# Key features on both halves of the partitions, scalings folded into constants, and another first product in the first MLP unit

## The chip, the cores and the metric

The kernel runs on one core of a Trainium2 chip. The metric is the device time of one execution in microseconds. Before the change it is 2621.38 us, the median of three runs from 2621.16 to 2624.04 us.

## The reference

There are two layers on an image x of two batches, 512 channels and 32 x 32 pixels. The first is a deformable attention with eight groups of 64 channels, followed by an MLP; the second is a plain attention over 1024 pixels. What matters here, cut down:

```python
# layer 0, per batch; 8 groups g of 64 channels; q is (64, 32, 32) in each group
q   = grouped_1x1(bn1(x), qw)
off = gelu(depthwise_6x6_stride_4(q) + b)             # (64, 8, 8)
off = tanh(einsum('bchw,oc->bohw', off, off_pw_w)) * 4.0   # o = x, y offset of 64 keys
vx, vy = gx + off[:, 0], gy + off[:, 1]
nx, ny = 2 * vx / 7 - 1, 2 * vy / 7 - 1
kv = grid_sample(bn1(x), (nx, ny))                    # bilinear at (nx + 1) * 16 - 0.5
k, v = grouped_1x1(kv, kw), grouped_1x1(kv, vw)
pos  = grid_q - (nx, ny)                              # grid_q = 2 * qx / 31 - 1, for x and y
bias = sign(pos) * log1p(abs(pos))                    # the "features" of a key
bias = relu(bias @ w1 + b1); bias = relu(bias @ w2 + b2)   # 2 -> 128 -> 128
bias = bias @ w3 + b3                                 # one number per pixel and key
out  = softmax(q.T @ k * 64**-0.5 + bias) @ v
x = x + out_w @ out + out_b
x = x + mlp_w2 @ gelu(mlp_w1 @ bn2(x) + mlp_b1) + mlp_b2   # 512 -> 2048 -> 512
# layer 1
q, k, v = linear(x); x = x + Wp @ (softmax(q k.T / sqrt(512)) v) + bp
```

pos has one x and one y part. Per group there are 32 pixel columns or rows times 64 keys of each, so 64 rows (32 for x, 32 for y) by 64 keys hold all features of a group. The 2 -> 128 -> 128 -> 1 network then runs on every pair of 1024 pixels and 64 keys.

## The kernel before

The program has four stages. Times in this section are those of the profiled execution.

**Head (0 to 37 us).** The weights of layer 1 are multiplied together on TensorE (`weights`, L589; products at L595), and beside that the first group pair goes through `chain(0)`.

**Main loop (37 to 1890 us, L886 to L930).** It has 256 steps, each with four keys of one group. A step does: the second half of the last step's sums (L888), moves and accumulating adds by DMA (L889), the broadcast load of the next table of features once in four steps (`load_tables`, L640, from the DRAM buffer `fdr`), the first network layer by one VectorE instruction (`st_layer1`, L676), the second by 32 TensorE matmuls with four ScalarE evictions behind them (`st_layer2`, L693, L703, L705), and its sum on VectorE (`st_sum`, L713). A group takes 16 steps.

Beside this runs background work, a generator `later()` (L556). It advances by one piece per step, up to its next `yield`: in each of the first 60 steps, then in three steps of four (L903 to L905). It prepares the next keys. `CHAINS` (L26) divides the eight pairs of groups into five chunks: two of one pair, then three of two. A pair is two groups of 64 channels on the two halves of the 128 partitions. For each chunk `later` runs

- `chain(ci)` (L320 to L477): the products for q, the depthwise convolution, Gelu into `gof` (L406), the products for the offsets (L418), Tanh into `th` (L428), `place_keys` (L439), the distances `pos` (L453), Abs, the log1p with a correction term (L456 to L469), and the write of the features to `fdr` (L470);
- `sample(ci)` (L479 to L554): the bilinear weights from `th` (L485 to L500), the gather as products with them (L513 to L533), and the products for k and v (L544, L547).

With K pairs in a chunk, n = 128 K. `th` is laid out as [partitions, 3, 2K groups, 64 keys]: the placed x, the placed y, and in the third part the values for the features, of all 2K groups side by side. The features themselves are made from `th[0:64, 2]` alone: 64 partitions (32 columns and 32 rows of pixels) by n elements.

`place_keys` multiplies by 4 and adds the key's grid place (L441), then scales by 2/7 and subtracts 1 (L446); L453 takes this from the query's grid place `gq`; L485 turns the placed keys into pixel coordinates. In chunk 0 the third part is placed first and the other two after the features have been sent off (L473).

There is also softmax work (`softmax_steps`, L831), in pieces too, one per step or so.

**Output projection and MLP (1890 to 2260 us).** The MLP runs in eight units, two batches times four quarters of the hidden layer. The products of a unit's first layer (`layer1`, L1089) are two-level Strassen-Winograd. `twice` (L141) lists them: three sets of seven products, each of which needs weights `w1x` and `w1e` (`w1e` are inner sums that are gathered by DMAs of GpSimd, `load_inner`, L986) and sums of the input `xb` and `xe`. A set's seven products lie at times 7g + t, by `STEPS`:

```python
    STEPS = ((0, 1), (1, 2), (3, 6), (4, 5), (6, 7), (9, 4), (12, 3))   # L139: (t, product)
```

so sets 0 to 2 start at 0, 7 and 14, and "fills" are put between by their own times. Products 1, 6, 7 and 4 are evicted by ScalarE (L166 to L176), and 2, 5 and 3 are added by VectorE. Some products share a PSUM bank: 6 and 7 (and 4) add on to the bank of product 1 once that has been read. The last fill, `second` (L1124, time 21), is the one plain product in `layer1` that needs no inner weights, w[0] by xb[0]: eight matmuls of 512 columns. It is added to c11, and Gelu makes the first quarter of the hidden layer from it. The other sets give the further quarters, by `done` (L1110). Then comes `layer2` (L1133). In the first unit of a batch, `xe` is still being summed by the fills `part(1)` and `part(2)`.

**Attention of layer 1 (2260 to 2622 us).** The change does not touch it.

[...] `tc.issue_after(i)` fixes where an instruction is put in that order. Instructions that are not ordered so are placed by the scheduler by their data.

Of the kernel before, what the change touches and what calls it, by code (L numbers as in the profile page):

```python
# [8 lines left out]
F32 = mybir.dt.float32  # L9
AF = mybir.ActivationFunctionType  # L10
ALU = mybir.AluOpType
# [3 lines left out]
P = 128  # L15
# [4 lines left out]
J = 64  # L20
NSL = 16
KT = 16
# [35 lines left out]
def conv_seq_kernel(ctx: ExitStack, tc: tile.TileContext, x, xt, kst, pst, cst, vec, wsm, outw, w1, w2, wl, wlt, brow, out):  # L58
    nc = tc.nc
# [30 lines left out]
    fdr = [dp.tile([2 * len(g), 4, 2 * W, KT], F32, name=f"fdr{i}") for i, g in enumerate(CHAINS)]  # L90
# [115 lines left out]
    ph = php.__enter__()  # L206
    with tc.tile_pool(name="lp", bufs=2) as lp:
# [45 lines left out]
        jg = cs[:, 0:192].rearrange("p (i j) -> p i j", i=3)  # L253
        gq = cs[:, 192:193]
        hb = ph.tile([P, 10], F32, name="hb")
        nc.gpsimd.tensor_scalar(hb[:, 0:9], cs[:, 193:202], -1.0, -0.5, ALU.mult, ALU.add)
# [16 lines left out]
        perm, place = pw_[:, 256:384], pw_[:, 384:512]  # L273
# [46 lines left out]
        def chain(ci):  # L320
            G = CHAINS[ci]
            K = len(G)
            (b, k0), n = G[0], 128 * K
            for i in range(K):
                k = k0 + i
# [5 lines left out]
                ps = flat("psq")  # L331
# [14 lines left out]
            acc = ph.tile([P, 3, K, 8, 8], F32, tag="acc", name="acc")  # L346
# [104 lines left out]
            ab, u, ln = (fe[0:64, i, :] for i in range(3))  # L451
            pos = thf[0:64, 2 * n : 3 * n]
            nc.vector.tensor_scalar(pos, pos, -1.0, gq[0:64], ALU.mult, ALU.add)  # L453
# [4 lines left out]
            if ci > 0:  # L458
# [4 lines left out]
            rc = acc.rearrange("p a k y x -> p (a k y x)")[0:64, 0:n]  # L463
# [15 lines left out]
        def sample(ci):  # L479
            G = CHAINS[ci]  # L480
            K = len(G)
            th = state[ci]
            gx = th[:, 0:2].rearrange("p i g j -> p (i g j)")

            nc.vector.tensor_scalar(gx, gx, 1.0, 16.0, ALU.add, ALU.mult)  # L485
            if ci > 0:
                yield

# [10 lines left out]
            nc.scalar.activation(hxf, th[:, 0].rearrange("p g j -> p (g j)"), AF.Abs, bias=hb[:, 0:1])  # L499
            nc.scalar.activation(hxf, hxf, AF.Relu, bias=1.0, scale=-1.0)  # L500
            yield
            gy = th[:, 1].rearrange("p (f k) j -> p f k j", f=2)
# [465 lines left out]
    with ExitStack() as top, tc.tile_pool(name="wp", bufs=1) as wp:  # L968
# [120 lines left out]
        def layer1(p, we, w, xb, xe, hm, others=()):  # L1089
# [40 lines left out]
            twice(mq, ((1, 6), (4, 7), (5, 3)), weights, moving, dest, done, ((21, second), *others))  # L1130
# [54 lines left out]
        for i, (b, p) in enumerate(units):  # L1185
# [11 lines left out]
            layer1(p, we, wa, xb, xe, hm, ((4, lambda: part(1)), (10, lambda: part(2))) if p == 0 else ())  # L1197
# [272 lines left out]
def _constants(np):  # L1470

    p = np.arange(P)
    kk = (p % 64)[:, None]
    j = np.arange(J)
    jx = np.broadcast_to((j % 8).astype(np.float32), (P, J))
    jy = np.broadcast_to((j // 8).astype(np.float32), (P, J))
    jm = np.where(kk < 32, jx, jy)
    gq = (np.float32(2.0) * (p % 32).astype(np.float32) / np.float32(31) - np.float32(1.0))[:, None]
    px = (p % 32).astype(np.float32)[:, None]
    py = ((p // 32)[:, None] + 4 * np.arange(8)[None, :]).astype(np.float32)  # L1480
    return np.ascontiguousarray(np.concatenate([jx, jy, jm, gq, px, py], axis=1), dtype=np.float32)
# [102 lines left out]
```

## Time and profile before

| | us |
|---|---|
| median of three runs | 2621.38 |
| the profiled execution, in all | 2623.41 |
| its span, from the first to the last instruction | 2621.6 |
| head, 0 to 37.2: TensorE / VectorE / ScalarE busy | 34.9 / 19.5 / 13.0 |
| main loop, 37.2 to 1895: the same | 1845.6 / 1805.7 / 1514.9 of 1857.8 |
| projection and MLP, 1895 to 2260 | 361.6 / 253.5 / 119.7 of 365.0 |
| layer 1, 2260 to 2621.6 | 355.1 / 232.6 / 98.1 of 361.6 |

The busy time of an engine is the time in which an instruction is executing on it; matmuls that overlap are counted once. Times below are microseconds from the start of the span. A line of the timeline has the start, the duration, the engine, the line of the kernel, the operation, output<-inputs, shapes, the number of instructions that are put together, and in brackets the time that the engine stood idle before it with what ended that. A line of the waits has who waited, for whom, and the sum, the number and the longest of these waits. A line of the table by stretch has the window, its length, then for TensorE, its weight loads, VectorE, ScalarE and GpSimd the busy time with the number of instructions, then the granted TensorE clock, the DMAs' share and GB/s.

The features' own operations in that execution: in a chunk of two the reciprocal L464 takes 1.74 us on 64 x 256, the others 0.2 to 0.42 us each, and L446 0.56 us on 128 x 768.

### The profile page before, as it was taken

Reading aid. Unit: us, or ns where it says so; the run is one execution under the profiler, and the core shown is the slowest. Engines: PE = TensorE matmul, PEld = TensorE weight load, DVE = VectorE, ACT = ScalarE, POOL = GpSimd, SP = SyncE. Lnnn points to the kernel's source line nnn. Section 1 sums busy time; section 2 is a strip of 40 time slices with the busy share of each in tenths; the row PEclk is TensorE's granted clock in tenths of the full one; section 3 lists DMA queues with packets and bytes.
Section 4 is the critical chain, followed back from the end, with each engine's and each line's share of the span. In section 5 each row is a group of like instructions: output and inputs, shape, how many; then the busy total and the mean of one; then the engine's idle time right before and its main releaser. Section 6 shows DMA issues by size and latency. Waiting matters only on the chain.

```text
span 2621.6 us, 48901 instructions
## 1 busy us (share of the span) xinstructions
PE 2597.2 (99%) x19648; PEld 1004.4 (38%) x19648; DVE 2311.3 (88%) x1462; ACT 1745.7 (67%) x2324; POOL 981.8 (37%) x1121
## 2 busy tenths in 40 slices
PE   9999999999999999999999999999999999999999
PEld 3332322233233233322233332332355665646556
DVE  7999999999999999999999999898776587666656
ACT  5887898888887888888887777777723242314041
POOL 1344544444445444444444454333332334200100
PEclk9999999999999999999999999999999999999999
DMA  5888988999999999899898999787777768400202
GB/s 190 174 191 186 213 183 184 195 200 201 189 191 194 188 204 195 180 190 201 186 202 181 196 193 193 163 181 166 160 198 162 153 139 177 90 16 0 73 0 57
DMA packets 177522, 428.27 MB, mean 163 GB/s; under 512 B 29936, under 2 KB 78208, under 8 KB 174608
## 3 DMA queue, kind: packets, MB, share of 16 engines
q0 software_dynamic: 107392, 273.09, 58.2%
q1 hardware_dynamic: 69472, 151.75, 17.4%
q8 instruction: 155, 2.54, 0.4%
q14 instruction: 71, 0.58, 0.1%
q10 hardware_dynamic: 432, 0.31, 0.0%
HBM read 82.16 MB, written 6.55 MB: 34 GB/s over the span
## 4 chain that ended last, share of the span: by engine, by line
PE 63%; DVE 12%; issue 10%; DMA 9%; POOL 4%; ACT 2%; DVEq 0%; SPq 0%; POOLq 0%; ACTq 0%
PE ps L693 37%; PE sw L1073 7%; PE sw L1234 7%; PE sw L160 6%; DVE h L676 5%; DMA u<-uc 3%; DVE ub L713 2%; POOL u L732 2%; PE sw L1332 2%; DMA u<-u 1%; PE psg L595 1%; DMA uc<-uc 1%; DVE hm L137 1%; DVE uo L713 1%; DMA w1e<-w1e 1%
## 5 line engine op out<-in xcount | busy, mean ns | idle before, releaser
L693 PE MATMUL ps<-h,cw 128*32 128x512 f32 x16384 | 1775.2, 593 | 10.8 <-ACT rx L703 7.7
L676 DVE CUSTOM_DVE_ANT_1 h<-ta,tb 128x4096 f32<-128x4096 f32 (+1 forms) x257 | 1130.1, 4398 | 20.8 <-PE ps L693 16.8
L693 PEld LDWEIGHTS ps<-h,cw 128*32 128x32 f32 x16384 | 525.7, 110 | 1229.3 <-issue 1132.9
L703 ACT ACTIVATE rx<-ps,sc 128x1024 f32<-128x1024 f32 x512 | 567.6, 1109 | 155.9 <-PE ps L693 97.5
L732 POOL DMA_DIRECT2D u<-u x397 | 410.1, 1516 | 14.6 <-DMA u<-ub 12.1
L705 ACT ACTIVATE ub<-ps,sc 128x1024 f32<-128x1024 f32 x256 | 307.8, 1202 | 84.0 <-PE ps L693 82.6
L713 DVE SCALAR_TENSOR_TENSOR ub<-rx,sc,ub 128x1024 f32<-128x1024 f32 x256 | 326.2, 1274 | 10.5 <-ACT ub L705 10.5
L715 POOL DMA_DIRECT2D uo<-ub x127 | 112.1, 883 | 584.2 <-DVE ub L713 536.7
L1073 PE MATMUL sw<-hm,w2t 128*128 128x512 f32 x448 | 193.9, 592 | 0.4 <-DVE hm L125 0.2
L705 ACT ACTIVATE uo<-ps,sc 128x1024 f32<-128x1024 f32 x128 | 153.9, 1202 | 42.4 <-PE ps L693 39.7
L713 DVE SCALAR_TENSOR_TENSOR uo<-rx,sc,uo 128x1024 f32<-128x1024 f32 x128 | 163.2, 1275 | 5.0 <-ACT uo L705 5.0
L732 POOL DMA_DIRECT2D u<-uc x126 | 126.8, 1269 | 19.4 <-DMA u<-uc 17.9
L715 POOL DMA_DIRECT2D uc<-ub x64 | 56.1, 877 | 199.7 <-DVE ub L713 158.9
L1073 PEld LDWEIGHTS sw<-hm,w2t 128*128 128x128 f32 x448 | 85.0, 190 | 104.8 <-issue 98.7
L137 DVE TENSOR_TENSOR hm<-hm,sw 128x512 f32<-128x512 f32 (+1 forms) x80 | 58.6, 737 | 74.4 <-PE sw L160 54.7
L715 POOL DMA_DIRECT2D u<-ub x64 | 55.4, 866 | 168.5 <-DVE ub L713 164.8
L732 POOL DMA_DIRECT2D uc<-uo x63 | 103.1, 1637 | 16.8 <-DMA uc<-uo 16.5
L732 POOL DMA_DIRECT2D uc<-uc x63 | 104.5, 1659 | 2.0 <-DMA uc<-ub 2.0
L1398 POOL DMA_DIRECT2D xs<-rs x6 | 7.2, 1200 | 258.1 <-DVE rs L137 258.1
L705 ACT ACTIVATE uc<-ps,sc 128x1024 f32<-128x1024 f32 x64 | 76.9, 1202 | 26.4 <-PE ps L693 16.6
L656 ACT ACTIVATE ta<-fb,vs 128x512 f32<-128x512 f32 (+1 forms) x65 | 89.2, 1376 | 6.5 <-DMA fb<-fdr 6.5
L732 POOL DMA_DIRECT2D u<-uo x63 | 83.3, 1322 | 24.7 <-DMA u<-uo 19.2
(294 smaller groups left out, 2624.9 us busy)
## 6 DMA issues: line engine op xcount, KB each, us to landing
uo<-ub POOLq DMA_DIRECT2D x127, 512.0 KB, 5.3
fb<-fdr SPq DMA_DIRECT2D x64, 512.0 KB, 6.1
u<-ub POOLq DMA_DIRECT2D x64, 512.0 KB, 6.7
uc<-ub POOLq DMA_DIRECT2D x64, 512.0 KB, 6.0
u<-u POOLq DMA_DIRECT2D x63, 256.0 KB, 7.0
u<-uo SPq DMA_DIRECT2D x63, 256.0 KB, 5.8
u<-uo POOLq DMA_DIRECT2D x63, 256.0 KB, 7.3
uc<-uc POOLq DMA_DIRECT2D x63, 256.0 KB, 8.0
```

The lines of the kernel that those rows point to most:

```text
L137: nc.vector.tensor_tensor(out, a, b_, op)
L160: nc.tensor.matmul(bank[:, e, :], w, x, start=(q in (1, 2, 5) and e == k == 0), stop=True, skip_group_check=True,)
L656: nc.scalar.activation(ta.rearrange("p j x -> p x j")[:, :, j0:j1], fb[:, 0, :, j0:j1], AF.Identity, bias=col("cb1"), scale=col("w1x"),)
L676: nc.vector._custom_dve(TENSOR_ADD_SAT, out=h1[:, y : y + step].rearrange("p y t x -> p (y t x)"), in0=a.unsqueeze(1).to_broadcast([P, ste ...
L693: nc.tensor.matmul(ps[32 * q : 32 * q + 32, h, :], cw2[:, 32 * z : 32 * z + 32], h1[:, 16 * h : 16 * h + 16, q, :], start=True, stop=True,)
L703: nc.scalar.activation(o, ps, AF.Relu, bias=sc[:, 4 + z : 5 + z])
L705: nc.scalar.activation(o, ps, AF.Relu, bias=sc[:, 4 + z : 5 + z], scale=sc[:, z : z + 1])
L713: nc.vector.scalar_tensor_tensor(r[1], r[0], sc[:, z : z + 1], r[1], ALU.mult, ALU.add)
L715: nc.gpsimd.dma_start(out=sums[s][1], in_=sums[s][3], accum_op=ALU.add)
L732: nc.gpsimd.dma_start(out=out, in_=in_, accum_op=ALU.add)
L1073: nc.tensor.matmul(ps[:, m, :], w[:, a, k, m * P : (m + 1) * P], x[:, b_, k, :], start=(k == 0), stop=(k == 1),)
L1234: nc.tensor.matmul(ps[:, m, :], w[:, a, k, c + m * P : c + (m + 1) * P], x[b_][:, k, :], start=(k == 0), stop=(k == nk - 1),)
```

## The change

**Layout of the features.** The six matmuls L418 become five: per half f of the partitions (groups of that half) one for x, one for y, both of 128 output rows, and one of 64 output rows for the features, which goes to the same half f of the partitions. `th` becomes [partitions, 5, m] with m = n / 2: x of both halves, y of both halves, and one slice whose lower and upper 64 partitions hold the feature values of the lower and upper groups. All operations of the features (L453 to L469) then run on 128 partitions by m elements instead of 64 by n. The write to `fdr` becomes two DMAs, one per half of the partitions.

**Constants.** The grid constants are scaled on the host, so that `place_keys` is one instruction per coordinate and gives pixel coordinates at once (128/7 times tanh plus 32/7 times the grid place); L446 and L485 go, and the `yield` behind L485 goes with it. The distances come in one instruction, -8/7 times tanh plus a constant that holds the query's grid place less that of the key. `gq` goes.

**First MLP unit.** `layer1` gets `early`, which is true for the very first unit alone. There the plain product is issued at time -1, ahead of all sets, and ScalarE copies it to the tile `r3` (in `first`); at time 13.5 `merge` adds it to c11 and issues the Gelu of that quarter. In the other seven units `second` stays at 21.

```diff
-        cs = ph.tile([P, 202], F32, name="cs")
+        cs = ph.tile([P, 201], F32, name="cs")
...
+            m = n // 2
             with tc.issue_after(marks[0]) if ci == 0 else nullcontext():
-                for i in range(3):
-                    for f in range(2):
-                        nc.tensor.matmul(
-                            ps[f][:, i * n // 2 : (i + 1) * n // 2],
-                            pw[i][64 * f : 64 * f + 64, :],
-                            gof[64 * f : 64 * f + 64].rearrange("p k j -> p (k j)"), start=True, stop=True,
-                        )
+                for f in range(2):
+                    r = slice(64 * f, 64 * f + 64)
+                    g = gof[r].rearrange("p k j -> p (k j)")
+                    for i in range(2):
+                        nc.tensor.matmul(ps[f][:, i * m : i * m + m], pw[i][r, :], g, start=True, stop=True)
+                    nc.tensor.matmul(ps[0][r, 2 * m : 3 * m], pw[2][r, r], g, start=True, stop=True)
             yield
...
-            th = ph.tile([P, 3, 2 * K, J], F32, tag="th", name="th")
-            thf = th.rearrange("p i g j -> p (i g j)")
+            th = ph.tile([P, 5, m], F32, tag="th", name="th")
             for f in range(2):
                 nc.scalar.activation(
-                    th.rearrange("p i (f k) j -> p f i (k j)", f=2)[:, f],
-                    ps[f][:, 0 : 3 * n // 2].rearrange("p (i m) -> p i m", i=3), AF.Tanh,
+                    th[:, f : 5 - f : 2, :], ps[f][:, 0 : (3 - f) * m].rearrange("p (i m) -> p i m", m=m), AF.Tanh,
                 )
...
             def place_keys(i0, i1):
                 for i in range(i0, i1):
+                    t = th[:, 2 * i : 2 * i + 2, :].rearrange("p f (k j) -> p (f k) j", j=J)
                     nc.vector.scalar_tensor_tensor(
-                        th[:, i], th[:, i], 4.0, jg[:, i].unsqueeze(1).to_broadcast([P, 2 * K, J]),
-                        ALU.mult, ALU.add,
+                        t, t, 128.0 / 7.0, jg[:, i].unsqueeze(1).to_broadcast([P, 2 * K, J]), ALU.mult, ALU.add
                     )
-                t = thf[:, i0 * n : i1 * n]
-                nc.vector.tensor_scalar(t, t, 2.0 / 7.0, -1.0, ALU.mult, ALU.add)
-
-            place_keys(2 if ci == 0 else 0, 3)
-
-            fe = ph.tile([P, 3, n], F32, tag="fe", name="fe")
-            ab, u, ln = (fe[0:64, i, :] for i in range(3))
-            pos = thf[0:64, 2 * n : 3 * n]
-            nc.vector.tensor_scalar(pos, pos, -1.0, gq[0:64], ALU.mult, ALU.add)
+
+            if ci > 0:
+                place_keys(0, 2)
+
+            fe = ph.tile([P, 3, m], F32, tag="fe", name="fe")
+            ab, u, ln = (fe[:, i, :] for i in range(3))
+            pos = th[:, 4, :]
+            posk = pos.rearrange("p (k j) -> p k j", j=J)
+            nc.vector.scalar_tensor_tensor(
+                posk, posk, -8.0 / 7.0, jg[:, 2].unsqueeze(1).to_broadcast([P, K, J]), ALU.mult, ALU.add
+            )
...
-            rc = acc.rearrange("p a k y x -> p (a k y x)")[0:64, 0:n]
+            rc = acc.rearrange("p a k y x -> p (a k y x)")[:, 0:m]
...
-            nc.sync.dma_start(
-                out=fdr[ci].rearrange("g c p j -> p (g c) j"), in_=ab.rearrange("p (g j) -> p g j", j=KT)
-            )
+            for f in range(2):
+                nc.sync.dma_start(
+                    out=fdr[ci][f * K : f * K + K].rearrange("g c p j -> p (g c) j"),
+                    in_=ab[64 * f : 64 * f + 64].rearrange("p (g j) -> p g j", j=KT),
+                )
...
-            gx = th[:, 0:2].rearrange("p i g j -> p (i g j)")
-
-            nc.vector.tensor_scalar(gx, gx, 1.0, 16.0, ALU.add, ALU.mult)
-            if ci > 0:
-                yield
-
+            gx = th[:, 0:4].rearrange("p i m -> p (i m)")
...
-        def layer1(p, we, w, xb, xe, hm, others=()):
+        def layer1(p, we, w, xb, xe, hm, others=(), early=False):
...
-            twice(mq, ((1, 6), (4, 7), (5, 3)), weights, moving, dest, done, ((21, second), *others))
+            def first():
+                ps = mq.tile([P, 2, 512], F32, tag="ps2", name="sw")
+                product(w, xb)(ps, 0, 0)
+                nc.scalar.copy(r3, ps)
+
+            def merge():
+                plus(c11, c11, r3)
+                gelu(0, c11)
+
+            plain = ((-1, first), (13.5, merge)) if early else ((21, second),)
+            twice(mq, ((1, 6), (4, 7), (5, 3)), weights, moving, dest, done, (*plain, *others))
...
-            layer1(p, we, wa, xb, xe, hm, ((4, lambda: part(1)), (10, lambda: part(2))) if p == 0 else ())
+            layer1(p, we, wa, xb, xe, hm, ((4, lambda: part(1)), (10, lambda: part(2))) if p == 0 else (), i == 0)
```

More of the change, by code (lines that the diff above doesn't have):

```diff
@@ L253, in conv_seq_kernel @@
         jg = cs[:, 0:192].rearrange("p (i j) -> p i j", i=3)
-        gq = cs[:, 192:193]
         hb = ph.tile([P, 10], F32, name="hb")
-        nc.gpsimd.tensor_scalar(hb[:, 0:9], cs[:, 193:202], -1.0, -0.5, ALU.mult, ALU.add)
+        nc.gpsimd.tensor_scalar(hb[:, 0:9], cs[:, 192:201], -1.0, -0.5, ALU.mult, ALU.add)
         uo = vp[:, NCH : 2 * NCH, :]
@@ L498, in sample @@
             hxf = hx.rearrange("p f k j -> p (f k j)")
-            nc.scalar.activation(hxf, th[:, 0].rearrange("p g j -> p (g j)"), AF.Abs, bias=hb[:, 0:1])
+            nc.scalar.activation(hxf, th[:, 0:2].rearrange("p f m -> p (f m)"), AF.Abs, bias=hb[:, 0:1])
             nc.scalar.activation(hxf, hxf, AF.Relu, bias=1.0, scale=-1.0)
             yield
-            gy = th[:, 1].rearrange("p (f k) j -> p f k j", f=2)
+            gy = th[:, 2:4].rearrange("p f (k j) -> p f k j", j=J)
             for i, (b, k) in enumerate(G):
@@ L1472, in _constants @@
     p = np.arange(P)
-    kk = (p % 64)[:, None]
     j = np.arange(J)
[L1475 to L1478, printed above, removed]
+    jx, jy = (np.broadcast_to(v.astype(np.float32), (P, J)) for v in (j % 8, j // 8))
+    jm = np.where((p % 64)[:, None] < 32, jx, jy)
+    grid = np.float32(2.0) * (p % 32).astype(np.float32)[:, None] / np.float32(31)
     px = (p % 32).astype(np.float32)[:, None]
     py = ((p // 32)[:, None] + 4 * np.arange(8)[None, :]).astype(np.float32)
-    return np.ascontiguousarray(np.concatenate([jx, jy, jm, gq, px, py], axis=1), dtype=np.float32)
+    place = np.float32(32.0 / 7.0)
+    return np.ascontiguousarray(
+        np.concatenate([jx * place, jy * place, grid - jm * np.float32(2.0 / 7.0), px, py], axis=1), dtype=np.float32
+    )
 def _order(np):
```

## The prediction

> **What bounds the kernel now.** I read the busy line of the page first, then the table of busy time by stretch, then TensorE's own waits inside the main loop (40 to 1895 us), and last the timelines at the two places that the change touches.
>
> ```profile
> PE 2597.2 (99%) x19648; PEld 1004.4 (38%) x19648; DVE 2311.3 (88%) x1462; ACT 1745.7 (67%) x2324; POOL 981.8 (37%) x1121
> ```
>
> ```profile
> 400.00:600.00 200.00, 197.31 (x1862) 60.37 (x1854) 198.54 (x110) 166.76 (x228) 93.96 (x113) 1.00 0.92 194
> ```
>
> ```profile
> PE ps L693 <- ACT rx L703: 7.7, 13, 1.9
> PE ps L693 <- DVE h L676: 1.6, 2, 0.8
> PE pkv L544 <- issue: 1.0, 1, 1.0
> PE ps L693 <- ACT ub L705: 0.7, 2, 0.4
> ```
>
> TensorE is busy 99%, VectorE 97 to 99% of the loop's stretches (second number: PE; fourth: DVE). But the loop's end is set by TensorE: in 1855 us it stands still for only 11.5 us (7.7+1.6+1.0+0.7 and two smaller rows of 0.3 and 0.2). So work taken off VectorE in the loop is worth at most its part in those 11.5 us.
>
> The transition into the first MLP unit, TensorE:
>
> ```profile
> 1951.94 1.89 PE L160 MATMUL sw<-xe,w1e 128*128 128x256 f32 x8
> 1956.02 1.13 PE L160 MATMUL sw<-xb,w1e 128*128 128x256 f32 x4 [2.19 <-DMA w1e<-w1e]
> 1956.98 4.44 PE L160 MATMUL sw<-xb,w1x 128*128 128x256 f32 x12
> 1961.26 1.03 PE L160 MATMUL sw<-xe,w1x 128*128 128x256 f32 x4
> ```
>
> ```profile
> 1953.80:1957.40 3.60, 1.41 (x7) 1.25 (x7) 0.21 (x1) 0.00 (x0) 3.15 (x4) 1.00 0.39 52
> 1957.40:1960.80 3.40, 3.40 (x9) 2.66 (x8) 2.33 (x3) 1.17 (x2) 1.08 (x2) 0.50 0.87 148
> ```
>
> The reader is to see two losses: 2.19 us in which TensorE waits for the last inner weight, and right after it 3.4 us at a granted clock of 0.50 (third number from the end), in which 12 passes need 4.28 us instead of 12 x 0.214 = 2.57: another 1.7 us. Together 3.9 us.
>
> ScalarE and VectorE in the head, and ScalarE at the end of that MLP unit:
>
> ```profile
> 20.63 1.28 ACT L435 ACT_TABLE_LOAD   x1
> 21.93 0.20 ACT L435 ACTIVATE hb<-ones 128x1 f32<-128x1 f32 x1
> 22.04 0.29 ACT L456 ACTIVATE fe<-th 64x128 f32<-64x128 f32 x1
> ```
>
> ```profile
> 21.40 0.27 DVE L453 TENSOR_SCALAR th<-th,cs 64x128 f32<-64x128 f32 x1
> 22.70 0.28 DVE L462 SCALAR_TENSOR_TENSOR fe<-fe 64x128 f32<-64x128 f32 x1
> 22.91 0.94 DVE L464 RECIPROCAL acc<-fe 64x128 f32<-64x128 f32 x1
> ```
>
> ```profile
> 1965.78 0.60 ACT L172 ACTIVATE hm<-sw 128x512 f32<-128x512 f32 x1 [2.00 <-PE sw L160]
> 1966.39 1.28 ACT L1092 ACT_TABLE_LOAD   x1
> 1968.70 1.33 ACT L1092 ACTIVATE hm<-hm,vs 128x512 f32<-128x512 f32 x2 [1.02 <-DVE hm L137]
> ```
>
> [...] there is no load between a Gelu and the copies after it. [...] half the columns is less than half saved: here 128x64 takes 0.21 us (L402) and 128x128 0.28.
>
> **Head (chunk 0 of the features).** Removed from VectorE before the distances: L446 and L453 (0.22 and 0.27); the rest shrinks. But the Abs at 22.04 doesn't wait for them: L453 ends at 21.67, and ScalarE is held by the table load and its dummy until 22.04. So this fusion gains nothing there. Behind it: two ScalarE steps 0.05 shorter each (128 to 64 columns), four VectorE operations 0.07 shorter each, and the reciprocal. That takes 0.94 us at 128 columns and 1.74 at 256 in the loop, so 6.2 ns per column and about 0.54 at 64: 0.40 gained. Sum 0.1+0.28+0.40 = 0.8 us, so the write of fdr starts at 24.1 instead of 24.90. It is two DMAs now; the load of the first table waits for the first alone (its half holds the first group), and the second is issued beside that wait. [...] So the tables come 0.8 to 0.9 earlier. What is late next is TensorE: its products L595 stand before the loop, the last starts at 36.30 and would release the loop at 36.73, while L693 starts at 37.25 because of h. Gain 0.5 us (0.3 to 0.7). The six matmuls L418 now go by half, not in turn between halves: 12 passes took 0.8 us and I keep 0.8 (0.2 either way, inside the range).
>
> **Loop (chunks 1 to 4).** For a chunk of two: before, by rows of the trace at 439 to 467 us, 0.42+0.75+0.56+0.34+0.41+0.41+1.74+0.22+0.40+0.41+0.41 = 6.1 us of VectorE. After: two placings 0.75, the fused one 0.23, and at 128x128 0.28+0.94+0.15+3 x 0.28 = 2.2; together 3.2. So 2.9 us less, three times, and 1.6 for the single chunk: 10.3 us off VectorE. TensorE's stalls that follow such features while VectorE is behind are those at 875 (0.36), 927 (0.26), 935 (0.99) and 1276 us (0.31): 1.9. I take 1.5. The yield that goes with L485 moves all later background work one step earlier per chunk, four steps at the end. By the order of the built program this parts two clumps (in step 147 a tensor reduce of features and the softmax maximum stood together, 4.1 us; they become 2.9 and 1.2 four steps apart), makes one denser (steps 52 and 53: 1.45 and 2.69 against 53 and 54: 0.59 and 2.60), and saves one table load of 1.28 us on ScalarE near 412 to 428 us, where TensorE loses 2.6. I take 0.5 for these. Loop: -2.0. It isn't bounded well: at the good end half of the 11.5 us goes (-6), at the bad end new collisions come (+8, below). On SP one issue of 0.69 to 1.18 us becomes two of about half; SP only moves data that lands several microseconds ahead of its use, cost zero; its effect if that cover is gone lies in the +8.
>
> **First MLP unit.** The product without inner weights (8 passes x 0.43 = 3.43 us) now comes first. It is moved, not added. TensorE then reaches the late weight at 1953.8+3.4 = 1957.3, after it has landed at 1955.97: the 2.19 us and the 1.7 us of half clock go, and some 0.3 us of small waits of the first steps, now behind the cover: -4.2. Its eviction (about 1.0 us on ScalarE) is beside matmuls.
> But the bias step (merge, then Gelu) now stands in the middle. On ScalarE the program has, in this order: the eviction of product 7 of set 1, that of product 4 of set 1, the table load, two Gelus, and only then the first copy of set 2. TensorE's product 6 of set 2 adds into the bank that this copy must have read. TensorE has product 4 of set 1 just before it. Call the end of that T: eviction starts at T+0.2 (1961.26+0.86 to 1962.33), 0.60; table load 1.28; Gelus 1.33; copy 0.58; about 0.1 of semaphores: T+4.1. Merge on VectorE is ready at T+0.1 and doesn't matter. So TensorE stands for 4.1 us. Before, the copy came ahead of all Gelus and nothing waited. An idleness of 4.1 us will drop the clock again: 0 to 2.4 us, I take 1.3. Unit: -4.2+4.1+1.3 = +1.2 (from -0.2 to +2.4). Behind the stall, the program puts layer 2's first product between the last ones of layer 1, and no later operand comes late by my reckoning: the next unit's inner weights had 7 us to spare before their last product, and lose 2.
>
> **Sum.** -0.5-2.0+1.2 = -1.3 us. The profiled execution took 2623.4 us (span 2621.6 and 1.8 around it), 2.0 over the median 2621.4; 2623.4-1.3 = 2622.1, on the median 2620.1.
>
> **Rivals.**
> (A) The forecast: one stall of the first unit is replaced by another. 2620, own range 2616 to 2625. Chance 0.56.
> (B) The cover works: the copy isn't late, or TensorE's wait for it is under a microsecond. For it: the stall removed is in the trace, clock and all. Against it: ScalarE's order as built. -0.5-2.0-4.2 = -6.7: 2614.7. Chance 0.21.
> (C) Slower: the earlier background work meets the softmax work in the loop. A collision of that kind at 414 to 423 us cost TensorE 2.6; three more, one for each chunk of two (steps 52 to 54 most likely), are 7.8 in place of the -2.0: -0.5+7.8+1.2 = +8.5: 2630. It decides once the loop's stalls exceed the present 11.5 us by 4.5. For it: VectorE, ScalarE and the DMAs are all nearly full there. Against it: 10 us less of VectorE work, and clumps that are mostly parted. Chance 0.23.
> That the change doesn't do what it says is excluded by the built program: shapes are halved and the product is first.
>
> **How the numbers follow.** A measurement tells 0.2% (5.2 us) from no change. Faster than 2616.1: most of B and a tail of A, 0.25. Slower than 2626.6: most of C, a little of A, 0.22. Within: 0.53. The range 2613 to 2630 holds A, most of B and about half of C.
>
> **What would show it.** First L693 at about 36.7; the sum of TensorE's waits in the loop near 9.5; no wait for w1e in the first unit, a wait of about 4 us for ScalarE's copy L166 in its place, followed by a clock of 0.50; the VectorE groups of th and fe 10 us lighter. A first unit without that wait makes B right; a loop with waits above 16 us makes C right.

## The result, and the profile after

The changed kernel takes 2631.41 us, the median of five runs (2628.26 to 2637.49), beside 2621.38 us for the kernel before (2620.89 to 2624.04). The ratio is 1.0041, with an interval of 1.0025 to 1.0057: some 10 us slower. The forecast was 2620 with a range of 2613 to 2630. The change's runs also lie further apart than those of before. The profiled execution is the fastest of the five, 2628.26 us with a span of 2626.5, and so 3.2 us under its median, while that of before (2623.41) lay 2.0 over its own. Between the two profiled executions there are therefore only 4.9 us, half of what lies between the medians.

In the loop and the MLP the lines of the new kernel have numbers that are lower by four: L693 is now L689, L703 is L699, L1092 is L1088. First the busy line of the page, then TensorE's waits in the main loop (who, for whom: sum, number, longest), then ScalarE, the issue of the features' writes and TensorE around 466 us, all from the trace of the changed kernel:

```profile
PE 2599.4 (99%) x19648; PEld 1013.1 (39%) x19648; DVE 2300.7 (88%) x1446; ACT 1745.6 (66%) x2324; POOL 985.2 (38%) x1121
```

```profile
PE ps L689 <- ACT rx L699: 10.8, 10, 2.8
PE ps L689 <- DVE h L672: 1.6, 2, 0.8
```

```profile
461.44 1.19 ACT L701 ACTIVATE ub<-ps,sc 128x1024 f32<-128x1024 f32 x1
466.04 0.72 ACT L488 ACTIVATE sg<-th,edge 128x512 f32<-128x512 f32 x1 [3.40 <-DMA fdr<-fe]
466.79 0.72 ACT L489 ACTIVATE sg<-sg,edge 128x512 f32<-128x512 f32 x1
467.42 1.10 ACT L699 ACTIVATE rx<-ps,sc 128x1024 f32<-128x1024 f32 x1
```

```profile
461.87 1.99 SPq L470 DMA_DIRECT2D fdr<-fe  x2
```

```profile
468.56 6.64 PE L689 MATMUL ps<-h,cw 128*32 128x512 f32 x60 [2.80 <-ACT rx L699]
```

The same chunk in the trace of before, where L492 is the first instruction of `sample` on ScalarE:

```profile
467.10 0.65 SPq L470 DMA_DIRECT2D fdr<-fe  x1
474.80 0.72 ACT L492 ACTIVATE sg<-th,edge 128x512 f32<-128x512 f32 x1
```

VectorE has lost 10.6 us in all, close to the 10.3 that were computed for the loop. TensorE's waits for L699 have nevertheless gone from 7.7 to 10.8 us, and the longest, 2.8 us at 468.56, has a cause that the trace of before does not have at all. ScalarE stands still for 3.40 us ahead of L488, the first instruction of `sample`, until the write of the features to `fdr` has landed (the DMA is complete), and the eviction L699 that TensorE needs is queued behind it. `sg`, which L488 writes, has the tag "fe": it takes the buffer of the features, and the DMA still reads that buffer. The two writes were issued from 461.87 us on; the second landed at 465.93. Before, the write landed at 473.88, and L492 did not wait. In chunk 4 there is a second such wait, 1.69 us at 1234.

TensorE in the head, before:

```profile
19.15 0.89 PE L418 MATMUL sim<-gof,ws 64*128 64x64 f32 x12
19.96 2.84 PE L595 MATMUL psg<-wl_s 128*128 128x512 f32 x6
```

The same place in the changed kernel, and then its first MLP unit (TensorE, ScalarE, and a stretch of 3.4 us behind the wait):

```profile
19.35 0.66 PE L420 MATMUL sim<-gof,ws 64*128 64x64 f32 x4
19.94 0.33 PE L421 MATMUL sim<-gof,ws 64*64 64x64 f32 x2
20.19 0.66 PE L420 MATMUL sim<-gof,ws 64*128 64x64 f32 x4
20.78 0.33 PE L421 MATMUL sim<-gof,ws 64*64 64x64 f32 x2
21.03 1.55 PE L591 MATMUL psg<-wl_s 128*128 128x512 f32 x3
```

```profile
1964.60 1.03 PE L160 MATMUL sw<-xe,w1x 128*128 128x256 f32 x4
1969.43 3.56 PE L160 MATMUL sw<-xe,w1e 128*128 128x256 f32 x8 [3.80 <-ACT hm L166]
```

```profile
1965.66 0.60 ACT L176 ACTIVATE hm<-sw 128x512 f32<-128x512 f32 x1 [1.99 <-PE sw L160]
1966.28 1.28 ACT L1088 ACT_TABLE_LOAD   x1
1967.57 1.33 ACT L1088 ACTIVATE hm<-hm,vs 128x512 f32<-128x512 f32 x2
1968.81 0.56 ACT L166 COPY hm<-sw 128x512 f32<-128x512 f32 x1
```

```profile
1969.20:1972.60 3.40, 3.17 (x8) 2.55 (x9) 0.69 (x1) 0.76 (x2) 0.00 (x0) 0.50 0.00 0
```

The offset products are six before and after (the account of the change says five): x, y and features for each half, of which the change makes the two for the features 64 columns wide. Each shows as two passes, twelve in all. They take from 19.35 to 21.03 us, 1.68 us, where before they took 0.81 (19.15 to 19.96). The first MLP unit shows what was forecast: the eviction L176, the table load, two Gelus, and only then the copy L166, with TensorE waiting 3.80 us for it and a granted clock of 0.50 after it (the number before the last two in the line of stretches).

From the first to the last matmul of the loop before takes 1851.2 us, after 1854.4. From the first product L595 (L591) to the loop it is 29.91 and 30.77.

### The profile page after: what moved, and what is told of

Read it like the earlier page. It is cut to its first block, busy times and chain, and to the rows that moved or that the text cites. A ratio compares the mean times of both kernels' runs of the same rounds, so it can differ in the third digit from the quotient of the medians.

```text
span 2626.5 us, 48896 instructions
## 1 busy us (share of the span) xinstructions
PE 2599.4 (99%) x19648; PEld 1013.1 (39%) x19648; DVE 2300.7 (88%) x1446; ACT 1745.6 (66%) x2324; POOL 985.2 (38%) x1121
## 4 chain that ended last, share of the span: by engine, by line
PE 77%; DVE 10%; issue 7%; DMA 3%; POOL 2%; ACT 1%; DVEq 0%; SPq 0%; ACTq 0%; POOLq 0%
PE ps L689 48%; PE sw L1069 7%; PE sw L160 7%; PE sw L1240 7%; DVE h L672 3%; DVE ub L709 2%; PE sw L1016 2%; PE sw L1338 2%; DMA u<-uc 2%; POOL u L728 1%; PE psg L591 1%; PE sim L819 1%; DVE uo L709 1%; DVE hm L137 1%; PE psx L1316 1%
## 5 line engine op out<-in xcount | busy, mean ns | idle before, releaser
L689 PE MATMUL ps<-h,cw 128*32 128x512 f32 x16384 | 1773.6, 592 | 13.5 <-ACT rx L699 10.8
L689 PEld LDWEIGHTS ps<-h,cw 128*32 128x32 f32 x16384 | 531.3, 110 | 1224.7 <-issue 1139.5
L699 ACT ACTIVATE rx<-ps,sc 128x1024 f32<-128x1024 f32 x512 | 568.0, 1109 | 146.8 <-PE ps L689 116.0
L728 POOL DMA_DIRECT2D u<-uc x126 | 126.6, 1282 | 16.2 <-DMA u<-uc 14.4
L137 DVE TENSOR_TENSOR hm<-hm,sw 128x512 f32<-128x512 f32 x79 | 57.6, 732 | 78.4 <-PE sw L160 53.5
L701 ACT ACTIVATE u<-ps,sc 128x1024 f32<-128x1024 f32 x64 | 77.1, 1204 | 25.5 <-PE ps L689 19.3
```

The lines of the kernel that those rows point to most:

```text
L137: nc.vector.tensor_tensor(out, a, b_, op)
L689: nc.tensor.matmul(ps[32 * q : 32 * q + 32, h, :], cw2[:, 32 * z : 32 * z + 32], h1[:, 16 * h : 16 * h + 16, q, :], start=True, stop=True,)
L699: nc.scalar.activation(o, ps, AF.Relu, bias=sc[:, 4 + z : 5 + z])
L701: nc.scalar.activation(o, ps, AF.Relu, bias=sc[:, 4 + z : 5 + z], scale=sc[:, z : z + 1])
L728: nc.gpsimd.dma_start(out=out, in_=in_, accum_op=ALU.add)
```

## The experiments

Each time is the median of its runs; the ratio is to the kernel before, run beside it on the same chip. All experiments compute the whole reference. The names in the headings are used further on.

### The parts, one at a time

**b_early:** the kernel before with the MLP part of the change alone (`first` at -1, `merge` with its Gelu at 13.5, in the first unit).

> The kernel before with the MLP part of the change alone. Theory 1 (three separate causes; the first MLP unit costs what its trace shows, a wait of 3.8 us and a half clock of 3.4 us in place of 2.19 us and a half clock of 3.4 us): 1.0 to 1.6 us over before, about 2622.8, with the loop as before (first L693 at about 37.3). Rival (the MLP part is most of the change's 10 us, by something after the first unit): 2628 to 2631.

2625.03 us, 1.0013 (1.0006 to 1.0020): +3.6 us. The 3.80 us wait is there and the loop is as before, so the rival falls, but the cost is twice what was expected. The half clock lasts 6.83 us here, where the changed kernel's profile had 3.41.

**a_noearly:** the changed kernel without that part.

```diff
-            layer1(p, we, wa, xb, xe, hm, ((4, lambda: part(1)), (10, lambda: part(2))) if p == 0 else (), i == 0)
+            layer1(p, we, wa, xb, xe, hm, ((4, lambda: part(1)), (10, lambda: part(2))) if p == 0 else ())
```

> The changed kernel without the MLP part (features alone). Theory 1: 1.4 us under the changed kernel, about 2630, with the half clock and the 2.19 us wait for w1e back. Rival (the MLP part is most of it): about 2622.

2627.92 us, 1.0030 (1.0018 to 1.0041), 3.5 us under the changed kernel: the same size from the other side. The wait for w1e is back with 1.38 us, but no half clock follows it, against what was expected. This is followed up below.

**a_yield:** the changed kernel with the yield put back in `sample`.

```diff
             gx = th[:, 0:4].rearrange("p i m -> p (i m)")
+            if ci > 0:
+                yield
```

> The changed kernel with the yield of L485 put back into sample, nothing else. Theory 1 (the loop's loss is ScalarE's wait, at the head of its queue, until the two fdr writes have landed, because sg takes the buffer of fe; one step more lets them land first): no ScalarE wait on fdr over 0.5 us, the sum of TensorE's waits in the loop at most that of before (10.7 us), the time 2624 to 2627. Rival (the loop loses by the layout itself, the two writes or the longer products, and the yield is nothing): 2630 to 2632.

2625.62 us, 1.0016 (1.0010 to 1.0023): 5.8 us less from one bare `yield`, the largest single part. No wait for fdr is left on ScalarE, and TensorE's waits are

```profile
PE ps L691 <- ACT rx L701: 6.4, 9, 1.9
PE ps L691 <- DVE h L674: 1.5, 2, 0.8
PE ps L691 <- ACT ub L703: 0.7, 2, 0.4
```

in all 8.6 us, below the 11.5 of before. The theory holds.

**a_inter:** the changed kernel with the six offset matmuls in turn between the halves.

```diff
-                for f in range(2):
-                    r = slice(64 * f, 64 * f + 64)
-                    g = gof[r].rearrange("p k j -> p (k j)")
-                    for i in range(2):
-                        nc.tensor.matmul(ps[f][:, i * m : i * m + m], pw[i][r, :], g, start=True, stop=True)
-                    nc.tensor.matmul(ps[0][r, 2 * m : 3 * m], pw[2][r, r], g, start=True, stop=True)
+                for i in range(3):
+                    for f in range(2):
+                        r = slice(64 * f, 64 * f + 64)
+                        g = gof[r].rearrange("p k j -> p (k j)")
+                        if i < 2:
+                            nc.tensor.matmul(ps[f][:, i * m : i * m + m], pw[i][r, :], g, start=True, stop=True)
+                        else:
+                            nc.tensor.matmul(ps[0][r, 2 * m : 3 * m], pw[2][r, r], g, start=True, stop=True)
```

> The changed kernel with the five offset matmuls in turn between the halves of the partitions again (x of both, y of both, features of both). Theory 1 (matmuls on different halves run beside one another only if they alternate): they take about 0.8 us instead of 1.7 in the head, the first L689 comes about 0.8 us earlier (37.4 to 37.6), and 0.8 to 1.5 us less in all, about 2630. Rival (the later start is the launch's jitter or the two writes): 38.3 again and no change, 2631.

2629.78 us, 1.0034 (1.0021 to 1.0046). The first matmul of the loop is at 37.24 instead of 38.32, and from the first L593 to it there are 29.94 us instead of 30.77, so the head is as much shorter as was expected; whether for the reason given is tested by b_byhalf. The time is 1.6 us less, but with runs from 2627 to 2633 this can't be told from no change, and the waits for fdr were longer in this trace (4.35 and 2.38 us). Repeated without them below.

### The yield: a wait, or work that comes one step early?

**a_hxfirst:** the changed kernel with `hx` (in the buffer of `acc`) made before `sg` (in that of `fe`). As many yields as the changed kernel.

```diff
+            hx = ph.tile([P, 2, K, J], F32, tag="acc", name="hx")
+            hxf = hx.rearrange("p f k j -> p (f k j)")
+            nc.scalar.activation(hxf, th[:, 0:2].rearrange("p f m -> p (f m)"), AF.Abs, bias=hb[:, 0:1])
+            nc.scalar.activation(hxf, hxf, AF.Relu, bias=1.0, scale=-1.0)
+            yield
             sg = ph.tile([P, 3, 2, K * J], F32, tag="fe", name="sg")
...
             yield
             nc.vector.tensor_tensor(sg[:, 2], sg[:, 0], sg[:, 1], ALU.mult)
-            hx = ph.tile([P, 2, K, J], F32, tag="acc", name="hx")
-            hxf = hx.rearrange("p f k j -> p (f k j)")
-            nc.scalar.activation(hxf, th[:, 0:2].rearrange("p f m -> p (f m)"), AF.Abs, bias=hb[:, 0:1])
-            nc.scalar.activation(hxf, hxf, AF.Relu, bias=1.0, scale=-1.0)
-            yield
```

> The changed kernel with the two steps of sample changed over: hx (in the buffer of acc, free by then) first, then sg (in the buffer of fe, which the fdr writes still read). As many yields as the changed kernel, so all background work keeps its early step; only the wait for the landing goes. Wait theory (all of the 5.8 us that the yield gave are ScalarE's wait for fdr): 2625 to 2626, TensorE's wait near 468 us (2.8) gone. Shift theory (they come from the background work being one step early, as in TensorE's wait of 2.3 us at 414 us behind the Gelu of gof): 2631, that wait unchanged. If both share: about 2628, with the wait near 468 gone and that at 414 still there.

2625.88 us, 1.0018 (1.0010 to 1.0025), as with the yield. TensorE's waits in its trace:

```profile
PE ps L689 <- ACT rx L699: 7.7, 8, 2.3
PE ps L689 <- DVE h L672: 1.6, 2, 0.8
```

The 2.8 us wait is gone; the 2.3 us at 414, which is the early background work, is still there and costs nothing that shows in the time. (Before has 0.54 and 1.67 us at that place, nearly the same sum.) So the loss was the wait for the landing, and the shift was not.

**b_noyield:** the kernel before with the yield behind L485 taken out, so with the old layout, one write and a full VectorE.

```diff
             nc.vector.tensor_scalar(gx, gx, 1.0, 16.0, ALU.add, ALU.mult)
-            if ci > 0:
-                yield
```

> The kernel before with the yield behind L485 taken out, nothing else: sg then follows the one fdr write of the old layout at the same distance as in the changed kernel. Theory (the yield alone makes the loop's loss, the new layout and the two writes do not): a ScalarE wait for fdr of 2 us or more in one or two of the chunks of two, and 4 to 6 us over before, 2625 to 2628. Rival (it takes the two writes to make the landing late): no such wait, 2621 to 2622.

2631.46 us, 1.0039 (1.0027 to 1.0052): +10.2 us. One `yield`, and more than the expected 4 to 6. ScalarE waits for fdr for 3.61 us at 236 and 5.52 at 469, and behind these TensorE for 1.84 and 4.17 us; this is ScalarE in its trace:

```profile
462.28 1.19 ACT L703 ACTIVATE ub<-ps,sc 128x1024 f32<-128x1024 f32 x1
468.99 0.72 ACT L490 ACTIVATE sg<-th,edge 128x512 f32<-128x512 f32 x1 [5.52 <-DMA fdr<-fe]
```

The two writes and the layout are not needed for the loss. Why it is larger than in the new layout was not tested. The trace shows two half clocks in the loop, of 3.41 us each, after waits of 2.27 and 4.17 us, and ScalarE stands still ahead of L490 in the other two chunks of the loop as well: 1.90 us at 853, until 0.08 us behind the landing, and 2.70 us at 1240, where the landing (1240.26) and L485 on VectorE (1240.40) end almost together. L485 is not there in the changed kernel, so not all of this loss need be the landing.

### The order of the offset matmuls

**b_byhalf:** the six matmuls of before by half instead of in turn.

```diff
-                for i in range(3):
-                    for f in range(2):
+                for f in range(2):
+                    for i in range(3):
```

> The kernel before with its six offset matmuls by half instead of in turn, nothing else. Theory (each pass then runs alone; 0.9 us more of TensorE in the head and in the single chunk, about 1.1 in each chunk of two, and TensorE is the bound): 3 to 5 us over before, 2624.5 to 2626.5. Rival (only the head counts, in the loop the passes fall into waits): 0.8 to 1.6 over, 2622 to 2623.

2621.89 us, 1.0001 (0.9993 to 1.0009): no change that can be told. The 3 to 5 us of the theory are outside the interval (-1.8 to +2.4 us), and the reason given, that matmuls of different halves run beside one another only when they alternate, is wrong. TensorE in the head of this kernel:

```profile
19.85 1.16 PE L418 MATMUL sim<-gof,ws 64*128 64x64 f32 x12
20.94 1.55 PE L595 MATMUL psg<-wl_s 128*128 128x512 f32 x3
```

Twelve passes in 1.09 us, by half, beside 1.68 for the changed kernel's twelve. What the changed kernel has besides is a change of shape inside each half, from weights of 64 x 128 to 64 x 64 and back. Its lines above show it: four passes from 19.35, then L421 only at 19.94, then L420 of the other half only at 20.19. By the starts in its trace each change costs time: the last L420 of a half starts at 19.73 and the first L421 at 19.94, 0.20 us later, where within one shape the passes of a half follow by 0.11 (0.16 behind the first L420). From the last L421 (20.04) to the next L420 (20.19) it is 0.15. Nor do the two halves overlap there: the second half's first pass starts at 20.19, after the first half's last (20.04). In b_byhalf it starts at 20.13, ahead of three passes of the first half (20.23 to 20.46) that stand before it in the program, so by its starts TensorE did not keep strictly to the program's order there. In turn, all of one shape stand together and there is one such change between the products, where by half there are three. The trace of the features alone in turn (f_clean, below) has

```profile
19.78 0.66 PE L421 MATMUL sim<-gof,ws 64*128 64x64 f32 x8
20.37 0.33 PE L423 MATMUL sim<-gof,ws 64*64 64x64 f32 x4
20.63 1.55 PE L595 MATMUL psg<-wl_s 128*128 128x512 f32 x3
```

twelve passes in 0.85 us.

**f_clean:** the features part alone, with the yield and the matmuls in turn; the first MLP unit as before. **f_yield:** the same with the matmuls by half.

> The features part alone with its two losses mended (yield back, offset matmuls in turn), first MLP unit as before. It asks what 10 us less of VectorE work in the loop are worth. By the sum of the runs so far (all mended 2617.0, the MLP part with its Gelu at 21 worth 2.7 by the trace): 2619.7, so 1 to 2.5 us under before. Rival (VectorE's work is all beside TensorE's, worth nothing): 2621 to 2622.

> The features part alone with the yield back, the offset matmuls by half as in the changed kernel; beside it stands the run with the matmuls in turn (2618.45). Theory (in the new layout the order by half costs TensorE 0.85 us in the head and 0.6 to 1.0 in each chunk, as the traces show, and TensorE is the bound): 3 to 4.3 us more, 2621.5 to 2622.7. Rival (only the head's part counts): 0.9 more, 2619.3.

2618.45 us, 0.9989 (0.9983 to 0.9996), and 2622.08, 1.0003 (0.9995 to 1.0011). So the new features are worth 2.8 us, and the order by half in the new layout costs 3.6, more than all of it. By the traces it is 0.83 us in the head (29.94 from the first L595 to the loop, 30.77 by half) and 3.2 in the loop (1847.5 and 1850.7 us from its first to its last matmul), where each chunk's passes take 0.6 to 1.0 us longer.

**a_yinter:** the changed kernel with the yield and the matmuls in turn, its first MLP unit as changed.

> The changed kernel with the yield back and the offset matmuls in turn; the first MLP unit as changed. Theory: 3 to 4.3 us under the one with the yield alone (2625.6), 2621.3 to 2622.6; and 4 to 5 us over the one with the Gelu at 21 as well (2617.0). Rival: 0.9 under, 2624.7.

2621.61 us, 1.0001 (0.9993 to 1.0009), 4.0 us under a_yield: the same answer with the changed MLP unit. Over f_clean it is 3.2, the MLP part once more.

### The first MLP unit

**a_gelu21:** the changed kernel with the Gelu of c11 apart from its sum. **b_early21:** the same edit in b_early.

```diff
             def merge():
                 plus(c11, c11, r3)
-                gelu(0, c11)
-            plain = ((-1, first), (13.5, merge)) if early else ((21, second),)
+            plain = ((-1, first), (13.5, merge), (21, lambda: gelu(0, c11))) if early else ((21, second),)
```

> The changed kernel with the first unit's Gelu of c11 apart from the merge: the sum stays at 13.5, the Gelu goes to 21, behind the evictions of products 1, 6 and 7 of set 2. Theory (the wait of 3.80 us is the table load and the two Gelus ahead of the copy of product 1, and the half clock is that wait's): both are gone, no half clock from 1940 to 2000 us, 6 to 8 us under the changed kernel, 2623 to 2625. Rival (the wait moves to the later evictions or to layer 2, which reads that Gelu): a wait of over 2 us within 15 us after, 2628 to 2632.

> The kernel before with the MLP part alone, its Gelu at 21. By the trace of the first unit (50.17 us before, 47.48 with the product first and the Gelu at 21): 2.7 us under before, 2618.7, with one wait of 1.2 us for ScalarE's copy and no half clock in the unit. Rival (later units or the loop's end give it back): 2621.

2627.24 us, 1.0023 (1.0015 to 1.0030), and 2620.86, 0.9998 (0.9990 to 1.0007). In both, the 3.80 us wait shrinks to 1.16, as in this line of b_early21, and no half clock follows:

```profile
1963.85 1.99 PE L160 MATMUL sw<-xe,w1e 128*128 128x256 f32 x8 [1.16 <-ACT hm L166]
```

4.2 us are won in either kernel (2625.03 to 2620.86 without the new features). The expectation of 6 to 8 was wrong in size, and b_early21 isn't 2.7 us under before but 0.4, which is no change. What remains of the wait is the copy behind the eviction of product 4 of set 1.

**before_again:** a second trace of the kernel before, since the first unit's half clock had not come back in a_noearly.

> The kernel before once more, for a second trace. Theory (the half clock in its first MLP unit was this one execution's, not the kernel's habit, since the unit takes 47.7 to 48.0 us without it in the kernels that keep the old first unit): the unit takes about 48 us here and shows no half clock; time 2621.4. Rival (it is the habit): half clock again, 50.2 us.

2621.38 us, 0.9999 (0.9991 to 1.0007). Its first unit:

```profile
1955.93 1.13 PE L160 MATMUL sw<-xb,w1e 128*128 128x256 f32 x4 [1.68 <-DMA w1e<-w1e]
1956.90 2.75 PE L160 MATMUL sw<-xb,w1x 128*128 128x256 f32 x12
```

The wait is 1.68 us and not 2.19, and the twelve passes behind it take 2.75 us and not 4.44: no half clock. From the unit's first product to that of the next it is 47.98 us here, 50.17 in the profile that the prediction used. The kernels that keep the old unit (a_noearly, f_clean, f_yield, b_byhalf, b_noyield) have waits of 1.17 to 1.90 us and no half clock either. With the product first and the Gelu at 13.5 the unit takes 51.7 or 53.0 us, as the half clock lasts 3.41 or 6.83 us; with the Gelu at 21 47.48.

### The scatter, and all three mended

**after_again:** the changed kernel once more.

> The changed kernel once more, for its spread and a second trace. If its scatter (2628 to 2637) is the landing of the fdr writes and the half clock that a wait of over 2 us in the loop can bring: the median within 2629 to 2633, ScalarE again waiting for fdr in the chunks of two, with other lengths than 3.40 and 1.69 us, and TensorE's wait of 2.3 us near 414 us the same. Rival (the scatter is the chip's, not this kernel's): the runs lie as close together as those of before.

2632.25 us, 1.0043 (1.0030 to 1.0056). The span of its trace is 6.1 us longer than that of the first, its loop starts no later, and its TensorE is busy for longer:

```profile
PE 2604.6 (99%) x19648; PEld 1014.5 (39%) x19648; DVE 2304.1 (88%) x1446; ACT 1746.5 (66%) x2324; POOL 979.5 (37%) x1121
```

```profile
466.00:469.20 3.20, 1.03 (x12) 0.12 (x4) 3.20 (x2) 2.48 (x4) 0.00 (x0) 1.00 1.01 238
469.30:472.70 3.40, 3.40 (x20) 0.84 (x24) 1.72 (x3) 2.48 (x3) 3.01 (x5) 0.50 0.71 177
```

ScalarE waits 2.78 and 1.64 us for fdr. The wait of 2.19 us that this makes for TensorE at 469 is followed by 3.4 us at a clock of 0.50 (second line), as is that of 2.32 at 414; the first trace had neither of these two half clocks, and the half clock in its first MLP unit lasted 3.41 us and not 6.83. So an execution of this kernel can be some 5 us longer by half clocks alone (TensorE is busy for 2604.6 us here and for 2599.4 in the first trace). That this is all of the scatter is argued from two traces, not shown.

**best_y:** the changed kernel with the yield, the matmuls in turn and the Gelu at 21. **best:** the same with `hx` first in place of the yield.

> All three mended in the changed kernel: the yield back, the offset matmuls in turn, the Gelu at 21. If the parts add up: 2625.6 (yield alone) less 0.8 (matmuls) less 6 to 8 (Gelu) = 2617 to 2619, below the kernel before. Rival (the parts mask one another): 2621 or more.

> As the one with all three mended, but with the two steps of sample changed over in place of the yield. Wait theory: 2617 to 2619 as well. Shift theory: 2622 to 2624, with TensorE's wait of 2.3 us at 414 us still there.

2617.01 us, 0.9983 (0.9977 to 0.9990), and 2618.30, 0.9988 (0.9980 to 0.9996). Both beat the kernel before, best_y by 4.4 us, and by 14.4 the change as it was made. best_y has no half clock before its last 4 us; the trace of best has one at 413, behind the wait of 2.29 us there, and one at 1891, behind a wait of 2.45. The two can't be told apart by their intervals.

## Why the prediction was wrong

From before to the change by kernels that differ in one edit: the new features in their good form (f_clean) -2.8; the matmuls by half (f_yield) +3.6; the MLP part (a_yield) +3.5; the yield gone (the change) +5.8. That is +10.1, and by the chain it must come to the measured 10.0; that the MLP part was also 3.6 in b_early and 3.2 in a_yinter over f_clean, and the matmuls 4.0 in a_yinter, is independent of it. Each step is uncertain by some 2 us.

- **The bound** was read rightly: TensorE sets the loop, and work off VectorE is worth no more than TensorE's waits. The features' groups on VectorE fell by 9.7 us in the loop (22.4 to 12.7; 10.3 were computed) and by 11.4 in all (26.6 to 15.2). f_clean gained 2.8 us of time, and TensorE's waits in its loop sum to 8.5 us where before has 11.5. The term of 1.5 for this was right within its uncertainty.
- **The yield is the step that failed most.** The prediction said of it: "moves all later background work one step earlier", weighed clumps that part and clumps that meet, and took 0.5 us of gain. The missing yield measured a loss of 5.8. Only where the work goes was asked, not what its first instruction waits for. The DMAs issued on SP, the write of fdr among them, were costed at zero since their data lands long before its use; but the use that counts is the buffer's next writer, `sg`. Behind the waiting instruction on ScalarE stood the evictions, behind those TensorE, which is the chain that the prediction followed for other waits. The trace of before had the numbers: write issued at 467.10, landed at 473.88, L492 at 474.80, so 0.9 us to spare, and the step that went is 7.2 us (1851.2 / 256). How much of the 5.8 is the wait itself varies between executions. With the yield and the same order of the offset matmuls the loop takes 1850.7 and 1850.8 us in two traces (f_yield, a_yield). Without it, it takes 1854.4 us in the trace with no half clock in the loop (the change), 1855.0 with one of 3.41 us (a_gelu21), 1856.1 with one of 6.83 (a_noearly) and 1857.1 with two of 3.41 (after_again).
- **The offset matmuls:** "12 passes took 0.8 us and I keep 0.8 (0.2 either way, inside the range)". They take 1.68 in the head and up to 2.0 in a chunk, five times, and cost 3.6 us. The term was mis-sized, for a change of the weights' shape that the diff shows in plain sight (`pw[2][r, r]`, 64 columns between products of 128; 0.20 and 0.15 us from one shape to the next in the head) and that was not priced.
- **The head:** nothing of the 0.5 us could be gained. The features' steps shrank much as computed: in the changed kernel the Abs takes 0.24 us, the reciprocal 0.55 and the product behind it 0.22, in the kernel before 0.29, 0.94 and 0.28. But the Abs starts at 22.89 instead of 22.04, behind the longer offset matmuls, and the write of fdr at 25.01 instead of 24.90. Its halves landed 2.3 us after their issue, the whole 2.2. "the last starts at 36.30 and would release the loop at 36.73", the prediction says of the products L595, and that missed a record: there is one more pass at 36.73, and TensorE had no gap ahead of the loop, as these two lines of before show. f_clean has 29.94 us from the first L595 to the loop where before has 29.91.

```profile
35.44 1.88 PE L595 MATMUL psg<-wl_s 128*128 128x512 f32 x4
37.25 1.07 PE L693 MATMUL ps<-h,cw 128*32 128x512 f32 x8
```

- **The first MLP unit:** mechanism, place and size of the new wait were right, 4.1 forecast and 3.80 measured: the table load 1.28, the two Gelus 1.33, the copy 0.56, and from its end to the matmul 0.06. Profile against profile the unit is 1.5 us longer (50.17 to 51.68), as forecast (+1.2). Yet the medians say +3.5, because the -4.2 had in it 1.7 us of half clock and 0.5 of waiting that the profiled execution of before had and most others haven't. The hint was on the page: that execution lay 2.0 us above the median, and the sum was carried over to the median as it stood. The half clock that came with the new wait, taken at 1.3, was the author's estimate from the one spell of 3.4 us behind the wait of 2.19. It is 1.7 us where it lasts 3.41 (in the change's profile eight passes take 3.39 us, 1969.43 to 1972.82; at the 0.216 us from start to start that such a pass has at a clock of 1.00 in the trace of before they take 1.73), and 1.3 more (53.0 - 51.7) where it lasts 6.83.
- **The rivals:** the slower one gave 2630 with a chance of 0.23, right in size and by another mechanism. It named collisions of the early background work with the softmax; a_hxfirst keeps those and is rid of the loss. The mended product (B) exists once the Gelu stands at 21, and it is worth 0.4 us alone, not 4.2, because the stall it removes is mostly 1.2 to 1.9 us without a half clock, and one of 1.16 takes its place.

## What to carry to other kernels

Where an edit takes a step out of a pipeline, list for each instruction behind it which buffer it writes and who still reads that buffer, outgoing DMAs above all. In this kernel a write to memory took 2.3 to 9.4 us from issue to landing, and ScalarE's wait of 3.40 us for one of them held the eviction queued behind it, and TensorE for 2.80 us with that. Keep matmuls with weights of one shape together: the order that mixes two shapes cost 3.6 us here (f_yield over f_clean). Before a stall in a profile is booked as gain, look into a second trace, or at how the profiled execution stands to the median, whether the kernel usually has it.

## What the runs showed of the hardware

The waits with which the granted clock fell to 0.50 (in the change the spell starts at 1969.20, 0.2 us ahead of the wait's end, in before at 1957.40, 1.4 us behind it): TensorE's 3.80 us in the first unit brought it in all seven traces that have it, for 3.41 us in four and 6.83 in three. The wait of 2.3 us at 414 brought it in five traces of eight. In the old first unit 2.19 us brought it once, and 1.17 to 1.90 us in six other traces never. In the loop 1.9 us at about 1814 did not in any. Near 470 us 2.19 us (after_again) and 4.17 us (b_noyield) brought it, and 2.12 us (a_gelu21), 2.80 us (the change) and 3.75 us (a_inter) did not. So no one length divides them: 2.19 us brought it in one execution, and 3.75 us did not in another. Each spell that such a wait brought was 3.41 us long or twice that.

DMA landings: the ten writes to fdr in the changed kernel took, from issue to landing,

```profile
DMA to landing us min/median/max: 2.3/3.7/9.4
```

for at most 32 KB each. Eight of them stand in the loop, where the DMA engines are busy at 0.89. The issue on SP did not divide in two either: one of 0.65 to 1.18 us became two, of 0.65 to 0.70 and of 0.93 to 1.42, so 1.7 to 2.1 us together.
